# Two-branch cross-attention on one core: a new written-out order of all engines and transfers, and new softmax forms for ten of sixty score groups

## The chip, the core and the metric

The kernel runs on one core of a Trainium2 chip. The metric is device time in microseconds (us), median of the timed runs. The engines are TensorE (PE in the profile, its weight loads PEld), VectorE (DVE), ScalarE (ACT), GpSimd (POOL) and SyncE (SP), whose queue issues nearly all transfers.

## What is computed

For x of shape (2, 2048, 640) and a context of shape (2, 154, 1024), in float32, with 20 heads of 32 columns:

```
text, ip = context[:, :77], context[:, 77:]
q  = heads(x @ Wq.T)
o1 = softmax(q @ heads(text @ Wk.T).T / sqrt(32)) @ heads(text @ Wv.T)
o2 = softmax(q @ heads(ip @ Wk_ip.T).T / sqrt(32)) @ heads(ip @ Wv_ip.T)
out = merge(o1 + o2) @ Wo.T + bo + x
```

Each of the two softmaxes has 77 keys; their results are added ahead of the output projection.

## The kernel before

Everything is kept transposed, columns on partitions and tokens along the free dimension. The work of attention is cut into ten **pairs** (batch b, chunk c of 128 columns, that is four heads), numbered q = 5b + c, and each pair into two **units** of 1024 tokens, u = 0 to 19, so pair q has units 2q and 2q + 1. A unit's scores are made in three **groups** s of 3, 3 and 2 tiles of 128 tokens. A group of 3 tiles has 12 x 2 = 24 rows of softmax on each partition (tiles x heads x text or ip, 77 keys each), a group of 2 tiles has 16. All eight PSUM banks are used: scores and attention take four at a time (a half), everything else one.

The order of the whole program is written out by hand in one list of words, `SCHEDULE`. The program goes through it once and each word records its instructions; each engine then runs its own instructions in that order, and waits only for data and for buffers to come free. So a place in the list sets the order within an engine and within SP's queue, not a time. The words that matter here:

- `q.u.h` (TensorE) queries of half h of a unit, five matmuls of 512 columns into the bank behind the @; `cq.u.h` copies them out on ScalarE, scaled. `k`, `v`, `ck`, `cv`: the same for keys and values.
- `Rs.u` scores of a group; `Ks.u` copies them from PSUM to the SBUF tile `pb` (ScalarE, four copies, L245); `M` the row maximum (VectorE, L281); `S` subtracts it (GpSimd, L295); `E` exponential (ScalarE, L301); `D` row sums (VectorE, L306); `I` reciprocal; `N` normalise (GpSimd, L316); `T` transpose in 32 x 32 blocks (VectorE, L323).
- `A.q` attention of a pair, 80 small matmuls (L332), which need all six transposes of the pair and its V, and `CA.q` copies it to `aT` on ScalarE.
- `VS.q.half` spreads V of a pair into the tile `v4`, eight small copies from SBUF to SBUF on SP's queue (L158); `LX` loads a block of x (1280 KB), `LK` and `LQ` weights, `LO` Wo, `SF` and `SS` fetch x for the residual and store a part of the output.
- `m`, `o`, `cm`, `co`: output projection of batch 0 in seven products of 2 x 2 blocks, with sums of weights (`W`) and of tokens (`G`) on GpSimd ahead of them and adds from PSUM into the tile `acc` on VectorE behind them.
- `F0` to `F32`, `p`, `z`, `V`, `X`, `Y`, `yz`: output projection of batch 1, at the end. 33 products of sums, each in two halves (L848). `V.w.j.e` adds 128 x 128 weights and `X.w.e` adds 128 x 1024 tokens, on VectorE (e = d) or GpSimd (e = p); `Y` adds a bank to a part of the output (VectorE, L792 and L794). A product that adds to a bank, or begins a new chain in it, needs the `Y` that read it last.

Each group has one of several softmax forms, by three sets. In `DIRECT` there is no copy: the maximum and the exponential read PSUM, four reductions for `M` (L284). In `DIRECT` and in `BIASED` there is no subtraction: the exponential takes the maximum as its bias, which makes it one instruction a row (L269). In `SUMMED` the exponential also sums its row on ScalarE (one more instruction a row in the trace), and `D` is left out.

The opening (loads, seven warm-up matmuls, three queries and the keys of chunk 0) is written ahead of the list.

Of the kernel before, what the change touches and what calls it, by code (L numbers as in the profile page):

```python
# [9 lines left out]
F32 = mybir.dt.float32  # L10
# [10 lines left out]
def kernel(  # L21
# [43 lines left out]
        (11, 0), (13, 0), (13, 2), (14, 0), (14, 2), (15, 1), (15, 2), (16, 2), (18, 1),  # L65
    }
    BIASED = {
        (2, 2), (3, 2), (4, 2), (5, 2), (6, 2), (7, 2), (9, 2), (11, 2), (12, 0), (12, 2), (18, 2), (19, 0),
        (19, 2),
    }  # L70
    SUMMED = {
        (4, 2), (6, 2), (11, 2), (12, 0), (12, 2), (13, 0), (13, 2), (14, 0), (15, 1), (15, 2), (18, 1),
        (18, 2), (19, 2),
# [480 lines left out]
    for t in range(2):  # L554
# [216 lines left out]
    for c, stages in enumerate(chains_of):  # L771
        for _, text in stages:
            for _, t in terms(text):
                for h in range(NH):
                    o = int(t[0]), NH * int(t[1]) + h
# [115 lines left out]
```

## Time and profile before

| What | before |
| --- | --- |
| timed runs, median (lowest to highest) | 497.72 us (497.66 to 498.04) |
| span of the profiled execution | 496.7 us |
| TensorE busy | 490.3 us (99%) |
| VectorE busy | 408.5 us (82%) |
| GpSimd busy | 362.5 us (73%) |
| ScalarE busy | 315.0 us (63%) |
| moved by DMA | 69.38 MB, 140 GB/s in the mean |
| granted TensorE clock | 1.000 |

For the profiled execution the profile gives the span, from its first to its last instruction, and no separate device time; the 1.0 us between the span and the median of the timed runs lies around it. A busy share is an average over the span; a wait is listed with the instruction that ended it.

### The profile page before, as it was taken

The numbers are of one execution on the slowest core, as the hardware profiler recorded it, in microseconds if no ns is written. First come the engines' busy times: TensorE is split into PE (matmuls) and PEld (weight loads), VectorE is DVE, ScalarE is ACT, GpSimd is POOL, SyncE is SP. The second block draws the span as 40 slices with busy tenths as digits, with TensorE's granted clock in tenths as the row PEclk, the third lists the DMA queues.
The fourth block names the chain that finished last, engine by engine and source line by source line (L and its number), as shares of the span: only waits on it lengthen the run. The fifth ranks groups of instructions, "written<-read, shape, count | busy, mean of one in ns | idle before, by whom it ended". The sixth has DMA issues, their size and how long they took to land.

```text
span 496.7 us, 10482 instructions
## 1 busy us (share of the span) xinstructions
PE 490.3 (99%) x4114; PEld 287.9 (58%) x4114; DVE 408.5 (82%) x412; ACT 315.0 (63%) x1021; POOL 362.5 (73%) x157
## 2 busy tenths in 40 slices
PE   8999999999999999999999999999999999999997
PEld 5676657657547556456647654755755675444442
DVE  0069989979979989969976896687999978898877
ACT  1165878978978778668999786587578966100000
POOL 0069978798888999989874858565899888284830
PEclk9999999999999999999999999999999999999999
DMA  8991440332360454886445177418525401420115
GB/s 259 356 246 40 132 120 1 106 93 69 92 213 3 132 178 132 274 273 237 158 152 191 58 244 210 133 57 246 174 69 171 127 23 43 149 84 1 43 73 223
DMA packets 67474, 69.38 MB, mean 140 GB/s; under 512 B 5473, under 2 KB 47201, under 8 KB 67425
## 3 DMA queue, kind: packets, MB, share of 16 engines
q1 hardware_dynamic: 66704, 68.00, 43.8%
q8 instruction: 32, 0.52, 0.5%
q10 hardware_dynamic: 720, 0.72, 0.4%
q14 instruction: 18, 0.14, 0.1%
HBM read 54.94 MB, written 10.49 MB: 132 GB/s over the span
## 4 chain that ended last, share of the span: by engine, by line
PE 92%; DMA 3%; SPq 1%; DVE 1%; POOL 1%; ACT 1%; issue 0%; POOLq 0%
PE bank L201 33%; PE bank L848 11%; PE bank L490 10%; PE bank L233 10%; PE bank L332 10%; PE bank L142 9%; PE bank L471 6%; PE bank L500 3%; DMA aT<-in_L_xattn_Wk_ip_dram 2%; DMA wq<-in_L_xattn_Wq_dram 2%; SPq L534 1%; POOL pb L316 1%; DVE den L306 0%; ACT pb L301 0%; SPq L132 0%
## 5 line engine op out<-in xcount | busy, mean ns | idle before, releaser
L316 POOL TENSOR_TENSOR pb<-pb,rden 128x1848 f32<-128x1848 f32 (+1 forms) x60 | 176.1, 2944 | 39.7 <-DVE rden L311 35.5
L201 PE MATMUL bank<-x,wq 128*128 128x512 f32 x400 | 180.4, 601 | 0.6 <-DMA x<-in_x_dram 0.5
L295 POOL TENSOR_TENSOR pb<-pb,mx 128x1848 f32<-128x1848 f32 (+1 forms) x38 | 119.3, 3152 | 51.8 <-DVE mx L281 51.5
L201 PEld LDWEIGHTS bank<-x,wq 128*128 128x128 f32 x400 | 74.1, 191 | 86.7 <-issue 80.8
L323 DVE STREAM_TRANSPOSE pb<-pb 128x1920 f32<-128x1920 f32 (+1 forms) x60 | 115.7, 1932 | 4.9 <-POOL pb L316 4.3
L281 DVE TENSOR_REDUCE mx<-pb 128x24 f32<-128x1848 f32 (+1 forms) x51 | 93.7, 1850 | 30.7 <-ACT pb L245 30.5
L245 ACT COPY pb<-bank 128x462 f32<-128x462 f32 (+1 forms) x204 | 87.2, 539 | 36.0 <-PE bank L233 35.4
L306 DVE TENSOR_REDUCE den<-pb 128x24 f32<-128x1848 f32 (+1 forms) x47 | 88.7, 1895 | 17.6 <-ACT pb L301 13.3
L301 ACT ACTIVATE pb<-pb 128x1848 f32<-128x1848 f32 (+1 forms) x38 | 64.2, 1696 | 17.8 <-POOL pb L295 17.5
L269 ACT ACTIVATE pb<-pb,mx 128x77 f32<-128x77 f32 x224 | 67.8, 364 | 0.3 <-DVE mx L281 0.2
L233 PEld LDWEIGHTS bank<-kT,qT 32*128 32x128 f32 x1280 | 45.4, 184 | 26.9 <-issue 15.6
L269 ACT ACTIVATE pb<-bank,mx 128x77 f32<-128x77 f32 x184 | 51.8, 386 | 9.3 <-DVE mx L284 9.3
L233 PE MATMUL bank<-kT,qT 32*128 32x154 f32 x1280 | 56.2, 305 | 0.3 <-ACT kT L559 0.3
L332 PE MATMUL bank<-pb,v 32*32 32x512 f32 x1600 | 55.2, 597 | 0.0
L142 PE MATMUL bank<-wo_ct,aT 128*128 128x154 f32 x320 | 45.6, 296 | 0.3 <-DMA aT<-in_L_xattn_Wk_ip_dram 0.3
L142 PEld LDWEIGHTS bank<-wo_ct,aT 128*128 128x128 f32 x320 | 42.9, 188 | 3.6 <-issue 2.2
L332 PEld LDWEIGHTS bank<-pb,v 32*32 32x32 f32 x1600 | 29.9, 103 | 22.8 <-issue 10.7
L211 ACT ACTIVATE qT<-bank 128x512 f32<-128x512 f32 x40 | 24.2, 619 | 22.1 <-PE bank L201 22.0
L471 PE MATMUL bank<-aT,wo_ct 128*128 128x512 f32 x80 | 36.1, 596 | 0.0
L269 ACT ACTIVATION_READ_ACCUMULATOR pb<-bank,mx 128x1 f32 x128 | 33.6, 267 | 0.0
L490 PE MATMUL bank<-aT,wo_ct 128*128 128x256 f32 x128 | 32.3, 385 | 0.0
L490 PEld LDWEIGHTS bank<-aT,wo_ct 128*128 128x128 f32 x128 | 23.7, 190 | 6.5 <-issue 3.0
(75 smaller groups left out, 434.4 us busy)
## 6 DMA issues: line engine op xcount, KB each, us to landing
x<-in_x_dram SPq DMA_DIRECT2D x20, 1280.0 KB, 6.7
out_dram<-acc SPq DMA_DIRECT2D x20, 256.0 KB, 2.3
x<-in_x_dram SPq DMA_DIRECT2D x18, 256.0 KB, 5.9
acc<-in_x_dram SPq DMA_DIRECT2D x16, 256.0 KB, 4.7
out_dram<-x SPq DMA_DIRECT2D x15, 256.0 KB, 2.0
v<-vS SPq DMA_DIRECT2D x160, 20.0 KB, 2.8
wq<-in_L_xattn_Wq_dram SPq DMA_DIRECT2D x9, 320.0 KB, 5.0
aT<-in_L_xattn_Wk_dram SPq DMA_DIRECT2D x5, 512.0 KB, 5.5
```

The lines of the kernel that those rows point to most:

```text
L142: nc.tensor.matmul(keys_in(out), loaded[n][:, k, :], cT[:, k, :, t, :], start=(k == 0), stop=(k == NCC - 1))
L201: nc.tensor.matmul(pq, wqs[q % 3][:, k, :], xs[place_of(u, h)][:, k, :], start=(k == 0), stop=(k == NC - 1),)
L233: nc.tensor.matmul(ps[g][:, ts(t, 2 * L)], qTs[(u, h)][g * D : (g + 1) * D, ts(st, P)], kT[g * D : (g + 1) * D, c, b].rearrange("p t l -> ...
L245: nc.scalar.copy(keys_of(u, s)[:, :, g], ps[g][:, : n * 2 * L].rearrange("p (n l) -> p n l", n=n))
L269: nc.scalar.activation(row, row if ps is None else rows_in(ps[g], n)[:, t, x], AF.Exp, bias=maxs[(u, s)][:, *one], accum_out=None if den i ...
L281: nc.vector.tensor_reduce(mx, rows_of(u, s), AX.X, ALU.max, negate=negate)
L295: nc.gpsimd.tensor_tensor(rows_of(u, s), rows_of(u, s), maxs[(u, s)].unsqueeze(3).to_broadcast([P, n, 2, L]), ALU.subtract)
L306: nc.vector.tensor_reduce(den_of(u, s), rows_of(u, s), AX.X, ALU.add)
L316: nc.gpsimd.tensor_tensor(rows_of(u, s), rows_of(u, s), rdens[(u, s)].unsqueeze(3).to_broadcast([P, n, 2, L]), ALU.mult)
L323: nc.vector.transpose(p, p)
L332: nc.tensor.matmul(pa[r][g * D : (g + 1) * D, :], v4s[q % 2][rows, g, k, :], zones[rows, :, g, k, :], start=(k == 0), stop=(k == NK - 1),)
L490: nc.tensor.matmul(part, w_of[m][:, kp, op], t_of(m, b, i)[:, kp], start=(op == kp == 0 and m in (1, 2, 5)), stop=(op == 1 and kp == 1 and ...
```

## The change

The list is written in another order, and the three sets that choose the softmax forms are changed. The words that don't belong to a form are the same, with the same engine for each `V` and `X`; some words use another PSUM bank. Buffers, shapes and the code of every word are the same. The sets are one line shorter and the list two lines, so line numbers behind them are lower: L158 becomes L157, L186 L185, L245 L244, and, behind the list, L792 becomes L789, L794 L791, L828 L825, L834 L831 and L848 L845.

```
     DIRECT = {
-        (11, 0), (13, 0), (13, 2), (14, 0), (14, 2), (15, 1), (15, 2), (16, 2), (18, 1),
+        (11, 0), (13, 0), (13, 2), (14, 0), (14, 2), (15, 1), (16, 2), (18, 1),
     }
     BIASED = {
-        (2, 2), (3, 2), (4, 2), (5, 2), (6, 2), (7, 2), (9, 2), (11, 2), (12, 0), (12, 2), (18, 2), (19, 0),
-        (19, 2),
+        (3, 2), (4, 2), (5, 2), (6, 2), (7, 2), (9, 2), (11, 2), (12, 2), (14, 1), (15, 2), (18, 0), (18, 2),
+        (19, 0), (19, 2),
     }
     SUMMED = {
-        (4, 2), (6, 2), (11, 2), (12, 0), (12, 2), (13, 0), (13, 2), (14, 0), (15, 1), (15, 2), (18, 1),
-        (18, 2), (19, 2),
+        (4, 2), (11, 2), (12, 2), (15, 1), (15, 2), (18, 2), (19, 2),
     }
...
     SCHEDULE = (
-        "R0.0@1 R1.0@0 K0.0 q.1.0@4 LK.5 K1.0 M0.0 M1.0 S0.0 R2.0@0 v.0.0@6 K2.0 cq.1.0 S1.0 M2.0 E0.0 v.0.1@0 LK.6 "
...
+        "R0.0@1 K0.0 R1.0@0 K1.0 q.1.0@4 cq.1.0 LK.5 M0.0 R2.0@0 K2.0 v.0.0@7 q.1.1@5 M1.0 M2.0 S0.0 S1.0 E0.0 D0.0 "
```

A pair (u, s) in a set is a unit and a group. Three places show how the engines' rows move.

**First, ScalarE at the scores of units 13 and 14.** `qT_16_0` is a copied query, `mx_14_2` and `mx_14_0` are the maxima of two groups of unit 14. Before:

```order
L269 ACTIVATE pb_89<-bank_7_74,mx_14_2_2543 128x77 x4
L301 ACTIVATE pb_89<-pb_89 128x12x154
L245 COPY pb_89<-bank_4_71 128x3x154
L245 COPY pb_89<-bank_5_72 128x3x154
L245 COPY pb_89<-bank_6_73 128x3x154
L245 COPY pb_89<-bank_7_74 128x3x154
L211 ACTIVATE qT_16_0_2605<-bank_1_68 128x512
L269 ACTIVATE pb_89,den_14_0_2634<-bank_4_71,mx_14_0_2629 128x77 x6
```

Now:

```order
L268 ACTIVATE pb_89<-bank_7_74,mx_14_2_2510 128x77 x4
L244 COPY pb_89<-bank_4_71 128x3x154
L244 COPY pb_89<-bank_5_72 128x3x154
L244 COPY pb_89<-bank_6_73 128x3x154
L244 COPY pb_89<-bank_7_74 128x3x154
L300 ACTIVATE pb_89<-pb_89 128x12x154
L210 ACTIVATE qT_16_0_2599<-bank_1_68 128x512
L268 ACTIVATE pb_89<-bank_4_71,mx_14_0_2582 128x77 x6
```

The exponential of group (13, 1), the row with 128x12x154, now stands behind the four copies of group (14, 1), and the exponential of (14, 0) has lost its sums (`den`).

**Second, SP's queue between the attention of pairs 7 and 8.** `v4_0` is the tile for V of even pairs and `v4_1` for odd ones, `x_1` one of the tiles for x. Before:

```order
L186 DMA x_2_84<-in_x_dram 128x5x512
L158 DMA v4_0_80<-vS1_95 32x160 x8
L461 DMA acc_87<-in_x_dram 128x2x256
L186 DMA x_0_82<-in_x_dram 128x5x512
L461 DMA acc_87<-in_x_dram 128x2x256
L467 DMA out_0_dram<-acc_87 128x2x256
L158 DMA v4_1_81<-vS1_95 32x160 x16
L467 DMA out_0_dram<-acc_87 128x2x256
L465 DMA out_0_dram<-res_88 128x512
L186 DMA x_1_83<-in_x_dram 128x5x512
```

Now:

```order
L157 DMA v4_1_81<-vS1_95 32x160 x8
L466 DMA out_0_dram<-acc_87 128x2x256
L185 DMA x_1_83<-in_x_dram 128x5x512
L460 DMA acc_87<-in_x_dram 128x2x256
L157 DMA v4_1_81<-vS1_95 32x160 x8
L466 DMA out_0_dram<-acc_87 128x2x256
L460 DMA acc_87<-in_x_dram 128x2x256
L157 DMA v4_0_80<-vS1_95 32x160 x8
```

The second half of pair 8's V (`VS.8.0`, the row with v4_0) stood ahead of both halves of pair 9's; now it stands behind them and behind the last x load.

**Third, the sums at the end, VectorE.** L828 (now L825) is a `V`, L834 (now L831) an `X`, L792 (now L789) a first `Y` or `yz`, L794 (now L791) a later `Y`. Before, from the four sums X.U, X.T, X.S and X.W in a row on:

```order
L834 TENSOR_TENSOR pb<-aT 128x1024 x4
L792 SCALAR_TENSOR_TENSOR x_83<-x_83,bo_sb,bank_71 128x512
L828 TENSOR_TENSOR pb<-pb,wo_ct 128x128
L834 TENSOR_TENSOR pb<-aT 128x1024
L792 SCALAR_TENSOR_TENSOR x_84<-x_84,bo_sb,bank_67 128x512
L792 SCALAR_TENSOR_TENSOR x_82<-x_82,bo_sb,bank_69 128x512
L792 SCALAR_TENSOR_TENSOR acc<-acc,bo_sb,bank_68 128x512
L792 SCALAR_TENSOR_TENSOR x_84<-x_84,bo_sb,bank_70 128x512
L828 TENSOR_TENSOR pb<-pb,wo_ct 128x128 x2
```

Now, from X.U and X.W on (the single row L831 is X.T, and the last row, wo_ct,pb, is V.H):

```order
L831 TENSOR_TENSOR pb<-aT 128x1024 x2
L789 SCALAR_TENSOR_TENSOR acc<-acc,bo_sb,bank_68 128x512
L789 SCALAR_TENSOR_TENSOR x_83<-x_83,bo_sb,bank_71 128x512
L789 SCALAR_TENSOR_TENSOR x_84<-x_84,bo_sb,bank_67 128x512
L831 TENSOR_TENSOR pb<-aT 128x1024
L825 TENSOR_TENSOR pb<-pb,wo_ct 128x128
L789 SCALAR_TENSOR_TENSOR x_84<-x_84,bo_sb,bank_68 128x512
L789 SCALAR_TENSOR_TENSOR res<-res,bo_sb,bank_74 128x512
L789 SCALAR_TENSOR_TENSOR x_84<-x_84,bo_sb,bank_70 128x512
L789 SCALAR_TENSOR_TENSOR x_82<-x_82,bo_sb,bank_69 128x512
L825 TENSOR_TENSOR pb<-wo_ct,pb 128x128
```

The sum X.T now stands among the adds from banks, and V.H, which was done far ahead of them, follows four of them.

And GpSimd at the same place, before:

```order
L828 TENSOR_TENSOR pb<-wo_ct,pb 128x128
L834 TENSOR_TENSOR pb<-aT 128x1024
L828 TENSOR_TENSOR pb<-wo_ct 128x128 x2
L834 TENSOR_TENSOR pb<-pb,aT 128x1024
L834 TENSOR_TENSOR pb<-aT,pb 128x1024
L834 TENSOR_TENSOR pb<-aT 128x1024
```

Now:

```order
L825 TENSOR_TENSOR pb<-pb,wo_ct 128x128 x2
L831 TENSOR_TENSOR pb<-aT,pb 128x1024
L825 TENSOR_TENSOR pb<-wo_ct 128x128
L825 TENSOR_TENSOR pb<-pb,wo_ct 128x128 x2
L825 TENSOR_TENSOR pb<-wo_ct,pb 128x128
L831 TENSOR_TENSOR pb<-aT 128x1024
```

The sum X.L (aT,pb) was the third long one, behind X.M and X.P; now it is the first of them, and four small sums stand between it and X.M.

122 rows, old and new, of the table SCHEDULE are left out of this document.

## The prediction

> **What bounds the kernel now.** I read the page first, then the waits of TensorE, then the chain of work that ended last. The page's engine shares and the chain's shares:
>
> ```profile
> span 496.7 us, 10482 instructions
> PE 490.3 (99%) x4114; PEld 287.9 (58%) x4114; DVE 408.5 (82%) x412; ACT 315.0 (63%) x1021; POOL 362.5 (73%) x157
> PE 92%; DMA 3%; SPq 1%; DVE 1%; POOL 1%; ACT 1%; issue 0%; POOLq 0%
> ```
>
> TensorE is idle for 496.7 - 490.3 = 6.4 us in all. Its waits, every one that the profile lists:
>
> ```profile
> PE bank L549 <- DVE pb L547: 1.1, 1, 1.1
> PE bank L201 <- DMA x<-in_x_dram: 0.5, 1, 0.5
> PE bank L233 <- ACT kT L559: 0.3, 1, 0.3
> PE bank L142 <- DMA aT<-in_L_xattn_Wk_ip_dram: 0.3, 1, 0.3
> PE bank L490 <- DVE acc L515: 0.2, 1, 0.2
> ```
>
> The first four (2.2 us) lie in the opening, ahead of the first word of the order, and its code stays. Three pieces of the chain in order of time (start, duration, what):
>
> ```profile
> 24.41 1.96 PE bank L233 x48
> ...
> 442.24 50.77 PE bank L848 x118
> 493.03 0.69 DVE acc L794
> ```
>
> The order begins at 24.41 with the first scores and ends with the last product at 493.0; behind that stand one add, one store and the closing, 496.7 - 493.0 = 3.7 us, which the new order keeps (its last two words are the same). So of the 6.4 us idle, 2.2 + 3.7 = 5.9 are out of the change's reach: 0.5 us are left for an order to win. Inside the products TensorE is paced by itself: 118 records are 59 products, 50.77 / 59 = 0.860 us each. The span of 496.7 belongs to the profiled execution; the median of the timed runs is 497.72, 1.0 us longer, and I carry that 1.0 over.
>
> **The change on TensorE itself.** It has the same 231 words, in almost the same sequence: up to pair 9's attention some fifteen words are swapped with a neighbour or two, and behind it the products are reordered more freely. What a change of kind costs (a group of full-height matmuls behind scores or attention) could differ, so I counted: 50 such changes into full height, 50 out of it and 20 between scores, before and now. TensorE's own work: 0.
>
> **The softmax forms.** Durations by form:
>
> ```profile
> L316 POOL TENSOR_TENSOR pb<-pb,rden 128x1848 f32<-128x1848 f32 x40 | 131.3, 3288 | 24.8 <-DVE rden L311 22.7 <-ACT aT L355 1.1 <-ACT pb L245 0.6
> L295 POOL TENSOR_TENSOR pb<-pb,mx 128x1848 f32<-128x1848 f32 x33 | 108.3, 3289 | 51.8 <-DVE mx L281 51.5
> L323 DVE STREAM_TRANSPOSE pb<-pb 128x1920 f32<-128x1920 f32 x40 | 86.3, 2160 | 3.7 <-POOL pb L316 3.2
> L306 DVE TENSOR_REDUCE den<-pb 128x24 f32<-128x1848 f32 x35 | 72.1, 2060 | 14.0 <-ACT pb L301 13.3 <-ACT pb L269 0.6
> L281 DVE TENSOR_REDUCE mx<-pb 128x24 f32<-128x1848 f32 x35 | 71.5, 2051 | 28.4 <-ACT pb L245 28.3
> L301 ACT ACTIVATE pb<-pb 128x1848 f32<-128x1848 f32 x33 | 58.0, 1765 | 16.4 <-POOL pb L295 16.2
> 225.00:250.00 25.00, 24.92 (x168) 15.33 (x167) 24.93 (x23) 22.44 (x87) 23.50 (x13) 1.00 0.56 183
> ```
>
> Six groups lose their sums on ScalarE: (12,0), (13,0), (14,0), (18,1) of 24 rows cost VectorE 2.06 each, (6,2) and (13,2) of 16 rows two thirds of that, 1.4: 11.0 us. (15,2) trades four reductions from PSUM for one from SBUF, some 0.5 less. VectorE: +10.5, from 82% to 84% of the span. GpSimd gets the subtractions of (2,2) and (12,0) back (2.2 + 3.3) and loses those of (14,1) and (18,0) (2 x 3.3): -1.1. ScalarE loses six sets of sums and the row-by-row exponentials of (2,2) and (12,0), gains those of (14,1) and (18,0) and four copies for (15,2): less work in all, and it is idle for 182 us. None of this is on TensorE's path while the engines keep ahead of it. The cover is thin in places: in the window row above (columns: PE, PEld, DVE, ACT, POOL busy) VectorE works 24.93 of 25 us, and (12,0)'s new sum falls right behind that stretch. If the cover goes, a late sum delays normalise and transpose, and the pair's attention waits. I followed two such chains.
>
> **Pair 6's attention (first order listing).** ScalarE now copies the scores R1.14 ahead of the exponential E1.13, which was the other way round; VectorE takes the maximum M1.13 later.
>
> ```profile
> 283.72 3.57 ACT L269 ACTIVATE pb<-bank,mx 128x77 f32<-128x77 f32 x16 [1.43 <-DVE mx L284]
> 287.60 1.07 PE L233 MATMUL bank<-kT,qT 32*128 32x154 f32 x24
> 288.69 2.00 ACT L245 COPY pb<-bank 128x462 f32<-128x462 f32 x4
> 292.55 2.27 DVE L284 TENSOR_REDUCE mx<-bank 128x6 f32<-128x462 f32 x4
> 301.17 5.52 PE L332 MATMUL bank<-pb,v 32*32 32x512 f32 x160
> ```
>
> R1.14 is computed from 287.60, so its copies end near 288.4 + 1.9 = 290.3. M1.13 follows M2.14 and an add on VectorE, say 285.4 to 287.4; S1.13 on GpSimd 3.3, to 290.8; E1.13 then 1.8, to 292.6: the copy in front of it costs nothing, because E1.13 is waiting for S1.13 anyway. Its sum 2.1 and reciprocal: 294.9. From there N1.13 takes 3.3, to 298.2, while VectorE does M0.14 (2.3, to 297.2) and T2.13 (1.5, to 298.7); T1.13 2.2 ends at 300.9. At the same time E0.14, unsummed now (16 such rows took 3.57, so 24 take 5.3), runs from 295.5 to 300.8. The attention, which overwrites the same banks and needs the transpose, starts at 301.17: 0.3 us to spare. Bounds: 0 if the chain is as short as this, 1.0 us if each of the six steps begins 0.2 later. I take 0, with the nearest row.
>
> **Pair 8's values (second listing).** Of the sixteen copies that spread V of pair 8, the eight of VS.8.0 move on SP's queue from ahead of pair 9's to the far end: behind a store, an x load, a fetch, pair 9's eight copies, a store and a fetch, two of which wait for a store to land. Each DMA counts:
>
> ```profile
> 341.09 0.38 SPq L186 DMA_DIRECT2D x<-in_x_dram  x1
> 341.52 6.74 SPq L158 DMA_DIRECT2D v<-vS  x8
> 358.74 10.89 SPq L158 DMA_DIRECT2D v<-vS  x16
> 364.53 0.68 DVE L521 TENSOR_TENSOR acc<-acc,bank 128x512 f32<-128x512 f32 x1
> 388.65 5.54 PE L332 MATMUL bank<-pb,v 32*32 32x512 f32 x160
> x<-in_x_dram SPq DMA_DIRECT2D x20, 1280.0 KB, 6.7
> out_dram<-acc SPq DMA_DIRECT2D x20, 256.0 KB, 2.3
> v<-vS SPq DMA_DIRECT2D x160, 20.0 KB, 2.8
> ```
>
> Eight copies take 5.4 to issue, or until the load issued just ahead of them has landed (341.09 + 6.7 is the end of the 6.74 row). The store in front waits for the add that ended at 365.2; allow 366. The x load follows at 366.5 and lands at 373.2. The fetch waits for the store's landing, 368.3; pair 9's copies then run to 374.2; the next store 374.7; its fetch waits 2.3, to 377; pair 8's eight copies run to 382.9 and land at 385.7. The attention that reads them starts at 388.65: 3 us to spare. Cost 0; if the queue is more than 3 us later, TensorE waits for each us beyond.
>
> **The closing products (third listing).** Here VectorE and GpSimd both add pairs of SBUF tiles, and those wait for each other:
>
> ```profile
> 436.11 0.28 DVE L828 TENSOR_TENSOR pb<-pb,wo_ct 128x128 f32<-128x128 f32 x1
> 436.31 1.22 DVE L834 TENSOR_TENSOR pb<-aT 128x1024 f32<-128x1024 f32 x1
> 436.48 1.37 POOL L828 TENSOR_TENSOR pb<-wo_ct,pb 128x128 f32<-128x128 f32 x1 [7.57 <-DVE pb L828]
> 469.41 4.66 POOL L834 TENSOR_TENSOR aT<-aT 128x1024 f32<-128x1024 f32 x2
> 472.73 1.50 DVE L828 TENSOR_TENSOR pb<-pb,wo_ct 128x128 f32<-128x128 f32 x1
> 428.85 2.31 ACT L359 COPY aT<-bank 128x256 f32<-128x256 f32 x8 [10.84 <-POOL pb L828]
> ```
>
> The small sum at 472.73 is the kind that took 0.28 at 436.11; it ended 0.15 after GpSimd's long add (469.41 + 4.66 = 474.07). GpSimd's small one at 436.48 ended behind VectorE's long one (437.5). The Trainium skill states the rule in "SBUF — State Buffer", section "Who interferes with whom": a VectorE instruction with two SBUF inputs contends with a GpSimd one that reads SBUF, and whichever came first holds the port for its whole length. By that rule the trace agrees, 1.50 against 0.28.
> Before, VectorE's long adds stood mostly where GpSimd was idle. Now GpSimd's run of long adds is placed otherwise, and VectorE's small sum V.H comes up beside one. Worked out: pair 9's copies end at 431.2; behind them VectorE does three long adds and a small one to 435.4, and GpSimd, held up twice, starts its add X.L near 435.7 and reads to 438. VectorE's X.T is ready at 437.8 and ends at 439.2. Four small GpSimd sums later X.M runs from 440.8 to 443.1. V.H, behind one more small sum and four bank adds of 0.63, is ready at 442 and waits 1.1. Four more adds then end at 445.9. TensorE reaches product 29's second half, which needs the last of them, at 429.1 + 1.0 + 3.4 + 14 x 0.86 = 445.5: 0.4 late. Bounds: 0 if V.H slips in ahead of X.M; 1.5 if the chain ahead is 0.6 later and two more products wait. I take 0.4, the worked value.
>
> **The sum.** 0 (TensorE) + 0 (forms) + 0 (pair 6) + 0 (pair 8) + 0.4 (ports) - 0.1 (part of the 0.5 idle) = +0.3: 497.72 + 0.3 = 498.0. A change under 0.2% (1.0 us) can hardly be told from none here.
>
> **Rivals.** *Slower by the ports:* V.H and the small sums behind it wait longer, VectorE's adds fall behind and bank after bank comes free late. For it speaks that both long waits in the trace are of this kind; against it that the later products have 0.5 to 1.6 us of room. Upper bound 1.5 of waits at the first two products, 0.5 behind: up to 499.7; it decides from 1.0 us of TensorE waits behind 437 us. Chance 0.16.
> *Slower by a late queue:* pair 8's values, or another chain like pair 6's, come late. It decides when the SP queue is 4 us behind my working, or three chains slip by 0.35. Price 1 to 3 us: 498.7 to 500.7. Against it: margins of 3 and 0.3 us are positive. Chance 0.12.
> *Faster:* the order takes out the 0.5 us of idle time and also gaps under 0.15 us that no row lists. Even 1.0 us would need twice the listed idle time: 496.6. Chance 0.07. The Trainium skill ("Perfetto Trace Analysis", section "Identifying the Most-Contended Engine") warns that TensorE's busy share says little on how near it is to its peak, and to look at the load share, here 58%. By that rule there would be room; the 0.860 us of every product, whatever it reads, shows none that an order could use.
> *No change that can be measured* is the forecast: 0.65.
>
> **Numbers.** The range of 8 in 10 leaves out most of faster and the late part of both slower cases: 497.0 to 499.4. Faster 0.07, same 0.65, slower 0.16 + 0.12 = 0.28.
>
> **What would show it.** TensorE's busy share again 99% and its waits behind 24.4 us under 1 us in sum; pair 6's attention near 301.2 and pair 8's near 388.7, without a wait for a DMA; VectorE's busy time near 419 us, less what waits are counted in; small VectorE sums of over 1 us behind 440, and a TensorE wait for a VectorE bank add near 445. The prediction is wrong if TensorE waits for a DMA in the attention part, or if its waits in the products pass 1 us.

## The result, and the profile after

| | before | changed |
| --- | --- | --- |
| timed runs, median (lowest to highest) | 497.69 us (497.52 to 498.04) | 501.88 us (501.40 to 504.16) |
| ratio, 95% interval | | 1.009 (1.0075 to 1.0105) |
| profiled execution, span | 496.7 us | 500.4 us |

The changed kernel is slower by 4.2 us, that is by 0.75% to 1.05%. The forecast of 498.0, with a range from 497.0 to 499.4, was wrong; slower had a chance of 0.28 in it. The changed kernel's times also spread more, over 2.8 us against 0.5. All medians of this document leave out three executions at a much lower granted clock (716.62 us at 0.656 of the kernel before, 718.93 at 0.659 and 519.86 at 0.946 of two experiments), and the changed kernel's slowest run, 504.16, had a clock of 0.996 where its others had 0.999 or 1.000.

These are the head of the changed kernel's profile, one row of its part on DMA queues (packets, MB, share) and the chain's shares by engine, and then the longest waits of TensorE (us in total, times, longest):

```profile
span 500.4 us, 10364 instructions
PE 491.3 (98%) x4114; PEld 288.6 (58%) x4114; DVE 423.5 (85%) x415; ACT 306.8 (61%) x905; POOL 366.1 (73%) x157
q8 instruction: 32, 0.52, 0.4%
PE 85%; DVE 6%; DMA 3%; POOL 2%; issue 1%; SPq 1%; ACT 1%; DVEq 0%; POOLq 0%
```

```profile
PE bank L232 <- issue: 1.6, 2, 1.1
PE bank L845 <- DVE x L789: 1.6, 2, 1.1
PE bank L548 <- DVE pb L546: 1.1, 1, 1.1
```

TensorE has 85% of the chain where it had 92, VectorE 6 where it had 1. Its waits in the opening are of the same kind as before, and two rows are new: 1.6 us in scores (L232) that the profile puts down to "issue", that is to nothing it can name, and 1.6 us in the closing products (L845) for adds from banks on VectorE.

To find the places, each TensorE word is followed from one trace to the other. The changed kernel is behind the kernel before (minus: ahead of it) by this much at the start of a pair's attention: pair 0 -1.06 us, pair 1 -0.98, pair 2 +0.09, pair 3 +0.31, pair 4 +1.65, pair 9 +1.10, and at the end +3.7. The first -0.8 is the opening, the same code in both (first scores at 24.41 us before, 23.58 after). So the loss has three places: 1.1 us behind pair 1's attention, 1.3 behind pair 3's, and 2.6 in the closing products; between pairs 4 and 9 half a microsecond is won.

**Place one and two, the scores behind the attention of pairs 1 and 3.** TensorE and SyncE of the changed kernel in order of time (start, duration, what; in brackets the idle time before it):

```profile
105.89 5.52 PE L331 MATMUL bank<-pb,v 32*32 32x512 f32 x160
105.99 0.37 SPq L191 DMA_DIRECT2D wq<-in_L_xattn_Wq_dram  x1
106.41 0.52 SPq L131 DMA_DIRECT2D aT<-in_L_xattn_Wk_dram  x1
111.34 1.05 PE L232 MATMUL bank<-kT,qT 32*128 32x154 f32 x21
112.95 0.53 PE L232 MATMUL bank<-kT,qT 32*128 32x154 f32 x3 [0.55 <-issue]
...
179.26 5.52 PE L331 MATMUL bank<-pb,v 32*32 32x512 f32 x160
179.36 0.37 SPq L185 DMA_DIRECT2D x<-in_x_dram  x1
184.71 0.80 PE L232 MATMUL bank<-kT,qT 32*128 32x154 f32 x15
186.56 0.55 PE L232 MATMUL bank<-kT,qT 32*128 32x154 f32 x9 [1.05 <-issue]
```

TensorE stops inside one word: of the 24 records of R0.5, 21 run and three come later, and of R0.9 15 run and 9 come later. The operands of all 24 are the same copies, so no operand can have come late in their midst. Counted in the trace among all TensorE records, the record behind the first stop is number 1986 and that behind the second number 3521: 1535 apart, six times 256 less one. The row of queue q8 says what has such a period: 32 packets of kind "instruction", 0.52 MB, 16 KB each, for 8321 TensorE records (matmuls, weight loads and 93 others), so one for some 256. This says that TensorE's instructions come by DMA in packets of 256, here called pages; the experiments below test it. The trace has each packet's start and length. The table sets them beside the TensorE record with which a page begins (number 194 modulo 256, to within one):

```
us             page before   packet of    packet     next page   next page begins
               begins        next page    has        begins      after landing
                             starts       landed
before,  pair 1   108.22        109.05      110.19      113.08       2.89
before,  pair 3   180.22        182.54      183.68      185.03       1.35
changed, pair 1   107.24        110.44      111.60      112.95       1.35
changed, pair 3   180.50        184.01      185.04      186.57       1.53
```

In these four rows a page's packet starts 0.8 to 3.5 us after the page ahead begins (where matmuls are long it can be ahead of that, by up to 7.4 us in the trace of before), and in the last three, where the page is only just in time or late, it is used 1.35 to 1.53 us after it has landed. Attention and scores use up a page in 4.7 to 4.9 us when nothing stops them. In the changed kernel the packets start 3.2 and 3.5 us after the page ahead begins. In the 1.3 us before that, 832 KB of weights and 1280 KB of x were issued (the SPq rows). In the kernel before it is 0.8 and 2.3 us.

**Place three, the closing products.** VectorE, GpSimd and TensorE of the changed kernel:

```profile
435.57 2.35 DVE L831 TENSOR_TENSOR pb<-aT 128x1024 f32<-128x1024 f32 x2
435.73 3.03 POOL L825 TENSOR_TENSOR pb<-pb,wo_ct 128x128 f32<-128x128 f32 x2 [5.90 <-DVE pb L825]
438.72 2.35 POOL L831 TENSOR_TENSOR pb<-aT,pb 128x1024 f32<-128x1024 f32 x1
439.81 2.35 DVE L831 TENSOR_TENSOR pb<-aT 128x1024 f32<-128x1024 f32 x1
443.72 2.34 POOL L831 TENSOR_TENSOR pb<-aT 128x1024 f32<-128x1024 f32 x1
443.86 1.40 DVE L789 SCALAR_TENSOR_TENSOR x<-x,bo_sb,bank 128x512 f32<-128x512 f32 x2
445.17 1.04 DVE L825 TENSOR_TENSOR pb<-wo_ct,pb 128x128 f32<-128x128 f32 x1
445.31 1.12 PE L845 MATMUL bank<-pb 128*128 128x512 f32 x2 [1.11 <-DVE x L789]
446.93 1.13 PE L845 MATMUL bank<-pb,wo_ct 128*128 128x512 f32 x2 [0.49 <-DVE x L789]
```

The GpSimd row at 435.73 holds two sums, V.U.2 (2.50 us; VectorE's X.U and X.W, the row at 435.57, are over at 437.92) and V.V.0 (0.45). So X.L starts only at 438.72, and X.T (439.81), a sum of 1.22 us by itself, takes 2.35 and ends 1.1 us after X.L. Six VectorE instructions later V.H (445.17) takes 1.04 us instead of 0.28; it ends just behind GpSimd's X.M (443.72). F20.1, the second half of product 20, waits for the second of the two adds at 443.86, which stand behind X.T, and F7.1 for the add behind V.H. Against the step of 0.86 us the losses are 1.27 at F20.1, 0.76 at F7.1, and 0.1 to 0.2 at five halves of products behind: 2.6 us.

### The profile page after: what moved, and what is told of

Same layout as the page of the kernel before. It is cut to its first block, busy times and chain, and to the rows that moved or that the text cites. A ratio compares the mean times of both kernels' runs of the same rounds, so it can differ in the third digit from the quotient of the medians.

```text
span 500.4 us, 10364 instructions
## 1 busy us (share of the span) xinstructions
PE 491.3 (98%) x4114; PEld 288.6 (58%) x4114; DVE 423.5 (85%) x415; ACT 306.8 (61%) x905; POOL 366.1 (73%) x157
## 4 chain that ended last, share of the span: by engine, by line
PE 85%; DVE 6%; DMA 3%; POOL 2%; issue 1%; SPq 1%; ACT 1%; DVEq 0%; POOLq 0%
PE bank L200 33%; PE bank L232 10%; PE bank L845 10%; PE bank L331 10%; PE bank L489 9%; PE bank L141 9%; PE bank L470 4%; PE bank L499 2%; DMA aT<-in_L_xattn_Wk_ip_dram 2%; DMA wq<-in_L_xattn_Wq_dram 1%; DVE pb L831 1%; POOL pb L315 1%; DVE x L789 1%; DVE den L305 1%; SPq L533 1%
## 5 line engine op out<-in xcount | busy, mean ns | idle before, releaser
L280 DVE TENSOR_REDUCE mx<-pb 128x24 f32<-128x1848 f32 (+1 forms) x52 | 95.4, 1844 | 35.9 <-ACT pb L244 35.9
L305 DVE TENSOR_REDUCE den<-pb 128x24 f32<-128x1848 f32 (+1 forms) x53 | 99.8, 1886 | 17.0 <-ACT pb L300 16.2
L244 ACT COPY pb<-bank 128x462 f32<-128x462 f32 (+1 forms) x208 | 88.5, 537 | 32.1 <-PE bank L232 31.6
L268 ACT ACTIVATE pb<-pb,mx 128x77 f32<-128x77 f32 x248 | 72.0, 373 | 3.2 <-DVE mx L280 3.2
L232 PEld LDWEIGHTS bank<-kT,qT 32*128 32x128 f32 x1280 | 45.6, 184 | 27.0 <-issue 16.3
L232 PE MATMUL bank<-kT,qT 32*128 32x154 f32 x1280 | 56.7, 305 | 1.9 <-issue 1.6
L268 ACT ACTIVATE pb<-bank,mx 128x77 f32<-128x77 f32 x168 | 39.0, 388 | 10.0 <-DVE mx L283 10.0
L791 DVE TENSOR_TENSOR x<-x,bank 128x512 f32<-128x512 f32 x36 | 23.9, 684 | 4.3 <-PE bank L845 3.6
```

The lines of the kernel that those rows point to most:

```text
L232: nc.tensor.matmul(ps[g][:, ts(t, 2 * L)], qTs[(u, h)][g * D : (g + 1) * D, ts(st, P)], kT[g * D : (g + 1) * D, c, b].rearrange("p t l -> ...
L244: nc.scalar.copy(keys_of(u, s)[:, :, g], ps[g][:, : n * 2 * L].rearrange("p (n l) -> p n l", n=n))
L268: nc.scalar.activation(row, row if ps is None else rows_in(ps[g], n)[:, t, x], AF.Exp, bias=maxs[(u, s)][:, *one], accum_out=None if den i ...
L280: nc.vector.tensor_reduce(mx, rows_of(u, s), AX.X, ALU.max, negate=negate)
L305: nc.vector.tensor_reduce(den_of(u, s), rows_of(u, s), AX.X, ALU.add)
```

## The experiments

Each experiment moves words of the changed kernel's list and nothing else, unless it is said otherwise. Times are medians; the kernel before, timed again beside each, had 497.6 to 497.7 us.

**The transfers alone.**

```
- q.5.1@2 S0.4 LK.14 LQ.5 E0.4 cq.5.1 A.1@1 ... LK.12 ... VS.2.0 M2.6
+ q.5.1@2 S0.4 LK.14 LK.12 E0.4 cq.5.1 A.1@1 ... VS.2.0 LQ.5 M2.6
- LX.11.0 LX.10.1 I2.8 v.4.1@5 VS.5.0
+ LX.11.0 I2.8 v.4.1@5 VS.5.0 LX.10.1
```

> The changed kernel with three transfers moved on SyncE's queue and nothing else: the weights LK.12 ahead of LQ.5, LQ.5 behind pair 2's first spread of V, and the x block LX.10.1 behind VS.5.0, so that none of them is issued in the first microsecond of the attention of pairs 1 and 3. Theory (instruction pages): TensorE's instructions come in pages of 256 by the same DMA engines; the page asked for 1.3 us into such an attention queues behind the fresh loads, lands 4.3 to 4.5 us after it was asked for instead of 2 to 3, and the scores R0.5 and R0.9 stop at the page's end for 1.1 and 1.4 us. Without the loads both stops go: 2.2 us less than the changed kernel, about 499.6. Rival (data): R0.5 and R0.9 wait for banks or operands that the new order of ScalarE and VectorE brings late; none of the three transfers feeds them, so no change, 501.9.

Measured: 499.80 us (499.44 to 500.14), 2.1 less than the changed kernel. TensorE's waits:

```profile
PE bank L845 <- DVE x L789: 1.6, 2, 1.1
PE bank L548 <- DVE pb L546: 1.1, 1, 1.1
PE bank L232 <- ACT kT L558: 0.3, 1, 0.3
```

The row with "issue" is gone, the one of the closing stays. The packets now start 0.9 us after the page ahead begins, in both places, and land 2.6 and 2.7 us before the next page is used.

**The reverse, on the kernel before.**

```
- LK.14 LK.11 M0.4 R1.4@1 q.5.1@1 T1.3
+ LK.14 M0.4 R1.4@1 q.5.1@1 LQ.5 LK.11 T1.3
- I2.5 LQ.5 ck.3.0
+ I2.5 ck.3.0
- K1.8 SF.0.2 T1.7 ... M0.9 LX.10.1 R2.9@0
+ K1.8 SF.0.2 LX.10.1 T1.7 ... M0.9 R2.9@0
```

> The reverse, on the kernel before: LQ.5 and LK.11 issued right behind pair 2's last queries, just ahead of pair 1's attention, and LX.10.1 right behind the queries that free its tile, just ahead of pair 3's; nothing else moves. Theory (instruction pages): the pages asked for at the start of these attentions now queue behind 832 and 1280 KB, land about 3 us or more after they were asked for (0.8 and 2.3 before), and R0.5 and R0.9 stop for about 1 us each: 498.6 to 499.6 where the kernel before has 497.6. Rival (data): earlier loads can only help or do nothing: 497.6.

Measured: 500.10 us, ratio 1.0047 (1.0034 to 1.006), 2.4 us slower, somewhat more than expected.

```profile
106.21 0.37 SPq L192 DMA_DIRECT2D wq<-in_L_xattn_Wq_dram  x1
106.64 0.52 SPq L132 DMA_DIRECT2D aT<-in_L_xattn_Wv_ip_dram  x1
112.85 0.53 PE L233 MATMUL bank<-kT,qT 32*128 32x154 f32 x3 [0.24 <-issue]
...
179.04 0.37 SPq L186 DMA_DIRECT2D x<-in_x_dram  x1
186.54 0.53 PE L233 MATMUL bank<-kT,qT 32*128 32x154 f32 x5 [1.11 <-issue]
```

The kernel before gets the same stops at the same instruction numbers, to within one. From pair 1's attention to pair 2's it loses 0.75 us against its own trace, from pair 3's to pair 4's 1.62, and nothing elsewhere. The packets land 1.28 and 1.32 us before the next page begins. Three transfers issued earlier cost 2.4 us, with no operand late: the data rival is out.

**Half a page more ahead.** Two runs put 128 TensorE instructions more into the opening, so that pages end elsewhere in the program.

```
- for _ in range(7):
-     nc.tensor.matmul(banks[0][:, :P], warm, warm, start=True, stop=True)
+ for _ in range(39):
+     nc.tensor.matmul(banks[0][:32, :32], warm[:32, :32], warm[:32, :32], start=True, stop=True)
```

> The changed kernel with 39 warm-up products of 32x32 by 32x32 in place of 7 of 128x128 by 128x128. Nothing else differs: all orders and all transfers stay, but every later TensorE instruction stands 128 places further on, half a page of 256. Theory (instruction pages): the pages' ends leave R0.5 and R0.9 and fall about 128 instructions earlier, into the queries or the attention itself; the page that is used up fastest is then asked for before the loads are issued. The stops of 1.1 and 1.4 us in R0.5 and R0.9 vanish; unless another page takes their place, 499.5, and any stop that is left lies a multiple of 256 instructions from the others, at a new place. Rival (data): both stops stay where they are, and the time with them, 501.9 plus or minus what the other warm-up does to the opening (0.5).

Measured: 504.39 us (504.04 to 505.19). Both expectations missed the time, and there is no trace of these runs that could tell why, so this experiment decides nothing. Then the large products came back:

```
+ for _ in range(32):
+     nc.tensor.matmul(banks[0][:32, :32], warm[:32, :32], warm[:32, :32], start=True, stop=True)
  for _ in range(7):
```

> The changed kernel with 32 small warm-up products (32x32 by 32x32) ahead of the 7 large ones, which stay: 128 TensorE instructions more, the clock warmed as before, all orders and transfers unchanged, and an opening that is 1 to 2 us longer. Theory (instruction pages): the stops in R0.5 and R0.9, which lie 6 pages of 256 apart, leave their places, since the pages now end half a page earlier in the program, in the queries ahead of the attention, and asked for before the loads are issued; about 1 to 2.5 us of stops less, and 1 to 2 of opening more. A stop that remains lies 128 instructions off the old ones, modulo 256. Rival (data): both stops stay in R0.5 and R0.9.

Measured: 505.97 us in one run, with an opening 2.0 us longer (pair 0's attention at 70.77 against 68.71). From there to pair 3's attention it keeps the distance to the kernel before, +0.99 to +1.16, and it keeps it to pair 4's (+1.33): the stops in R0.5 and R0.9 are gone. There is one stop without a named cause, inside pair 4's attention:

```profile
209.71 0.41 SPq L185 DMA_DIRECT2D x<-in_x_dram  x1
212.90 4.90 PE L331 MATMUL bank<-pb,v 32*32 32x512 f32 x134
218.88 1.13 PE L331 MATMUL bank<-pb,v 32*32 32x512 f32 x26 [1.07 <-issue]
```

The record behind it is number 4290, nine times 256 behind number 1986. The packet of that page started 3.4 us after the page ahead began, while 1284 KB of data were moved, and landed 1.46 us ahead of its use. No order of data has changed, and the stop has gone where the page's end went; the packets are 33 now, for 8449 records.

The time is worse than expected. In the traces it is 3.8 us more than the changed kernel: 2.1 more in the opening, 2.2 less in the two places, 1.6 more between the attention of pairs 4 and 5, and 2.3 more in the closing. There, just behind the two stops for VectorE, the granted clock was 0.5 for 3.4 us (from 448.70 on), and the products F29.0 and F29.1 lost 0.75 and 0.85 us where the changed kernel's lost 0.1 each. Why the clock fell here and not behind the same stops in the changed kernel's trace, no run settles.

**The closing: two words moved.**

```
- F20.0 X.L.p@9 V.V.1.d V.M.0.p ... Y6.1.10 V.H.0.d yz.1 ... Y2.1.31 F29.0 V.W.0.p V.S.0.d
+ F20.0 V.V.1.d V.M.0.p ... Y6.1.10 yz.1 ... Y2.1.31 V.H.0.d F29.0 V.W.0.p X.L.p@9 V.S.0.d
```

> The changed kernel with two words of the closing products moved and the same work: GpSimd's long sum X.L behind four small sums, just ahead of X.M, and VectorE's small sum V.H behind five adds from banks. Theory (shared port): X.T (2.35 us where 1.22 is its own length) and V.H (1.04 instead of 0.28) no longer meet GpSimd's long adds, VectorE's adds come 1.1 us earlier at F20.1 and 1.9 us earlier at F7.1; both stops of TensorE go, and the steps of 0.95 behind them: 2.2 us less, 499.7. Rival (backlog): VectorE simply has too many sums ahead of its adds from banks; the order of GpSimd changes nothing, and 0.28 us of V.H is all that goes: 501.6.

Measured: 500.16 us, 1.7 less than the changed kernel; the profile still has a stop of 1.55 us in R0.9 and only 0.2 us of waits for VectorE. As the pages' stops differ between traces (0.55 and 1.05 us in the changed kernel's, one of 1.55 here), the words were also moved on top of the first experiment's kernel.

> The changed kernel with both edits at once: the three transfers of the first experiment out of the attention's start, and the two words of the closing products moved. Theory (pages and port, two separate causes that add up): 499.8 of the first experiment less 1.6 to 2.3 of the closing = 497.5 to 498.2, level with the kernel before, with no stop in R0.5 and R0.9 and none at F20.1 and F7.1. Rival (something else in the new order or in the softmax forms costs time as well): 0.5 us or more above the kernel before is left, and TensorE shows waits elsewhere.

Measured: 497.95 us, ratio to before 1.0004 (0.9995 to 1.0013). TensorE's waits behind the opening:

```profile
PE bank L845 <- DVE x L789: 0.2, 1, 0.2
```

The losses against the step of 0.86 are 0.5 us in all where the changed kernel has 2.6. One after the other the edits take out 2.1 and 1.85 us, 3.9 of 4.2, and the rest can't be told from nothing. The moved words take out nearly as much with the pages' stops (1.7) as without them (1.85), so the two causes stand side by side.

**V.H alone**, on the changed kernel and then on the first experiment's.

```
- Y6.1.10 V.H.0.d yz.1 ... Y2.1.31 F29.0
+ Y6.1.10 yz.1 ... Y2.1.31 V.H.0.d F29.0
```

> The changed kernel with VectorE's small sum V.H alone moved behind five adds from banks; GpSimd's order is as in the changed kernel. Theory (shared port): the stop at F20.1 stays at 1.1 us, because the add that it needs stands ahead of V.H and behind X.T; the stop at F7.1 and the slower steps behind it go, since V.H no longer waits for X.M: 0.8 to 1.0 us less, 501.0. Rival (backlog): 0.28 us less at most, 501.6.

Measured: 501.82 us (500.93 to 504.36), not separable from the changed kernel, because the runs of both scatter over more than the effect; what makes them scatter stays open, since one run of each was traced. The trace has the stop at F20.1 (1.10 us) and none at F7.1.

> The first experiment's kernel (499.8), with VectorE's small sum V.H alone moved behind five adds from banks. Theory (shared port): the stop at F20.1 stays at 1.1 us, that at F7.1 goes, since V.H no longer waits for GpSimd's X.M: 0.8 to 1.0 us less, 498.9. Rival (VectorE has too much ahead of its adds, and the port adds nothing): 0.28 us less at most, 499.5.

Measured: 499.05 us, 0.75 less: nearly the 0.8 to 1.0 of the shared port and well over the rival's 0.28. The stop at F20.1 is there as before (1.10 us), the 0.49 at F7.1 is not:

```profile
442.99 1.12 PE L845 MATMUL bank<-pb 128*128 128x512 f32 x2 [1.10 <-DVE x L789]
443.95 1.02 PE L845 MATMUL bank<-pb,wo_ct 128*128 128x512 f32 x2
```

**X.L alone**, on the first experiment's kernel; VectorE's order is untouched.

```
- F20.0 X.L.p@9 V.V.1.d ... V.W.0.p V.S.0.d
+ F20.0 V.V.1.d ... V.W.0.p X.L.p@9 V.S.0.d
```

> The first experiment's kernel (499.8), with GpSimd's long sum X.L alone moved behind four small sums, just ahead of X.M; VectorE's order is untouched. Theory (shared port): X.T takes about 1.25 instead of 2.35 us, the stop of 1.1 us at F20.1 goes, and V.H waits for one of the two long GpSimd sums for 0.2 to 1.0 us: 1.2 to 1.8 less, 498.0 to 498.6. Rival (VectorE has too much ahead of its adds): its work and its order are the same, so no change, 499.8.

Measured: 497.94 us, 1.9 less, a little more than expected. X.T and V.H on VectorE, and X.L on GpSimd:

```profile
437.80 1.28 DVE L831 TENSOR_TENSOR pb<-aT 128x1024 f32<-128x1024 f32 x1
441.83 0.45 DVE L825 TENSOR_TENSOR pb<-wo_ct,pb 128x128 f32<-128x128 f32 x1
439.77 2.36 POOL L831 TENSOR_TENSOR pb<-aT,pb 128x1024 f32<-128x1024 f32 x1
```

VectorE's work and order are the same, and 1.9 us go because one long sum of GpSimd starts 3.1 us later (counted from pair 9's attention): VectorE's load alone is not the cause. Moving V.H as well gains nothing more (497.95 with both words), so the two effects of 1.9 and 0.75 don't add up: with X.L moved, V.H takes 0.45 us and hardly waits.

**The heads and tails exchanged.** First the kernel before up to pair 9's last transpose, and the changed kernel's order behind it (forms as before):

> The kernel before up to the last transpose of pair 9, forms included, and the changed kernel's order behind it. Theory (the closing order is a cause of its own): the stops at F20.1 and F7.1 of about 1.1 and 0.5 us and the slower steps behind them, 2.0 to 2.6 us in sum: 499.6 to 500.2. Rival (VectorE comes into the closing late because of the 10 us of added sums in the attention part): without these sums the closing costs less than 0.5 us, 497.6 to 498.1.

Measured: 498.62 us, ratio 1.0017 (1.0008 to 1.0027), 0.9 us slower: less than half of what the theory gave, and more than the rival's 0.5. The port's waits are there (X.T 1.88, V.H 1.05 us), and one stop:

```profile
PE bank L850 <- DVE x L794: 0.5, 1, 0.5
```

Here VectorE comes out of the last transpose 0.5 us ahead of pair 9's attention, in the changed kernel 0.06 us ahead, and the next sums are not held up by GpSimd (V.T.0 0.47 against 1.05 us); so the add that F20.1 needs is in time. The stop of 1.27 us in the changed kernel needs both, the meeting with X.L (without it, under the same head, there is no stop at F20.1) and a VectorE that comes late from the attention part. Then the opposite, the first experiment's head with the closing order of before behind it:

> The changed kernel's order and softmax forms up to the last transpose of pair 9, with the three transfers moved as in the first experiment, and behind it the order of the kernel before, whose closing products have no stop of TensorE. Theory (two causes, nothing else; the new forms and the new attention part cost nothing): 497.3 to 497.8, at or just under the kernel before; the profile shows no wait behind the opening over 0.3 us. Rival (the new attention part or its added sums bring VectorE into the closing later, and that costs time under any closing order): 498.2 or more, with a wait for VectorE between 440 and 450 us.

Measured: 498.83 us, ratio 1.0025 (1.0016 to 1.0034). The theory's 497.3 to 497.8 missed, and the rival had the time and the wait right. GpSimd, VectorE and TensorE:

```profile
429.94 7.55 POOL L829 TENSOR_TENSOR pb<-pb,wo_ct 128x128 f32<-128x128 f32 x3 [3.11 <-DVE pb L829]
431.73 4.62 DVE L835 TENSOR_TENSOR pb<-aT 128x1024 f32<-128x1024 f32 x4
440.97 1.13 PE L849 MATMUL bank<-pb 128*128 128x512 f32 x2 [1.14 <-DVE acc L793]
```

V.U.2, the first of the three GpSimd rows, came up at 429.94, when VectorE had begun its run of sums without a gap, and ended at 436.66: 6.72 us for a sum that takes 0.45. In the kernel before it is done at 428.1, ahead of the run. Counted from the start of pair 9's attention, the add that TensorE waits for ends 2.1 us later than before. VectorE comes out of the last transpose 0.45 us later, its first sum takes 1.47 us instead of 0.35 beside a long one of GpSimd, and later it waits 0.52 for a GpSimd sum that stands behind V.U.2. So the late head and the port have a part in it together. The rival's "under any closing order" goes too far: the same head with the two words moved runs level with the kernel before (497.95).

**Three more small sums moved**, on the kernel with both edits:

```
- X.J.d@4 V.R.0.d Y6.1.21 ... Y7.1.21 V.W.1.d ... Y7.0.21 V.S.1.d ... F13.0 V.M.1.d F2.0
+ X.J.d@4 V.R.0.d V.W.1.d V.S.1.d V.M.1.d Y6.1.21 ... Y7.1.21 ... Y7.0.21 ... F13.0 F2.0
```

> The kernel with both edits (497.95), and three of VectorE's small sums (V.W.1, V.S.1, V.M.1) moved up behind V.R.0, into a stretch in which GpSimd has no long add. Theory (shared port): the three take 0.28 us each instead of 0.91, 1.18 and 1.12; of the 0.4 to 0.5 us that TensorE still loses at F24.0 and F13.0 most goes: 497.5, at or just under the kernel before. Rival (these waits cost nothing, since nothing that TensorE needs stands behind them): 497.95.

Measured: 497.69 us, ratio to before 1.0004 (0.9995 to 1.0013). The three sums take 0.29 us each, as expected, and the loss at F24.0 is shorter by 0.2 us. The median is 0.26 lower, but the ratio to the kernel before beside it is the same 1.0004, so theory and rival can't be told apart. No version here beats the kernel before; three are level with it.

## Why the prediction was wrong, step by step

*What bounds the kernel.* That TensorE's stream sets the time, and that only 0.5 us could be won, held. But the step "TensorE's own work: 0" took the stream as given. It had no term for what feeds TensorE with instructions, and no rival for it: the waits of before show none, since there the pages came in time (at pair 3 with the same 1.35 us as in a stop). The sign "TensorE waits for a DMA in the attention part" came true only in this hidden form. This omitted term is 2.1 us by the first experiment. The transfers were costed by their readers alone, at pair 8; the ones that cost time are others, which nobody was waiting for. A smaller misreading is the 1.0 us carried over from the span: each timed run here is 1.7 to 1.9 us longer than its own span, so the traced execution of before was itself some 0.8 us slower than the median. It moves nothing in the sum.

*The softmax forms: 0.* With the two causes taken out, the changed forms run level with before (1.0004), so by themselves they cost nothing that can be measured. But the same closing order lost 1.2 us in the trace behind the old head and 2.6 behind the new one. The head thus has a share in the loss at the closing; whether through the forms or through the order, no run separates. The 24-row sums went from 35 to 39:

```profile
L305 DVE TENSOR_REDUCE den<-pb 128x24 f32<-128x1848 f32 x39 | 80.4, 2061 | 16.4 <-ACT pb L300 16.2
```

VectorE was busy for 423.5 us where 419 was forecast; sums held up by GpSimd, which count as busy, are in it: with both edits it is 421.3, with the three small sums moved as well 419.4.

*Pair 6 and pair 8: 0.* Right. Their attention, without idle time ahead of it:

```profile
302.74 5.52 PE L331 MATMUL bank<-pb,v 32*32 32x512 f32 x160
389.72 5.52 PE L331 MATMUL bank<-pb,v 32*32 32x512 f32 x160
```

It starts later than the forecast 301.2 and 388.7 by what was lost earlier; with both edits it starts at 300.40 and 387.37. No wait of TensorE for a transfer of data is listed there.

*The closing products: 0.4.* The mechanism was right and the size wrong: 2.6 us in the trace, of which moving two words takes away 2.1 (1.85 in the medians). The step that failed is "GpSimd, held up twice, starts its add X.L near 435.7". It started at 438.72. Of these 3.0 us, 1.1 are the delay with which pair 9's attention began, and 1.9 are the closing's own. The row quoted from before shows a small GpSimd sum that waits for one long add; V.U.2 ahead of X.L waited for two that follow each other without a gap (2.50 us), and in the exchanged tail for a whole run (6.72). From there all shifted: X.T met X.L, which the working had nearly past each other, and the first product to stop was F20.1, not F29.1, where 0.1 us was lost. V.H's wait behind X.M, forecast at 1.1 us, measured 0.8. A wait for a bank add near 445 was named in advance and came, at 445.31, but at another product and behind another sum: that the times agree is luck.

*The rivals.* Slower by the ports (0.16) was the nearest: it was to decide from 1.0 us of TensorE waits behind 437 us, and there are 1.6. It gave at most 499.7, and could not reach 501.9 without the pages. The sign "its waits in the products pass 1 us" was the right one for this part; the one on transfers named no page of instructions. The opening, set at no change, differs by up to 1.5 us between profiles of the same code (first scores from 22.9 to 24.4 us), more than the 0.2% on which the chances were split.

## What to carry to other kernels

When all engines look hidden and TensorE's program is long, look at its instruction pages. Keep large transfers out of the microsecond or two in which a stretch of many short matmuls begins, because the next page comes late behind them, and read "issue" at distances of a multiple of 256 in the instruction count as the sign. Where VectorE and GpSimd hold each other up, place the sums by runs, not one by one: a short GpSimd sum that came up inside a run of VectorE sums waited here for the rest of the run. An order that is level by its sums can be 1% apart by such meetings, so compare orders with these two alone undone before judging the rest.

## What the hardware showed that was not expected

TensorE's instructions came in 32 packets of 16 KB, one for 256 instructions, and landed late when transfers of 0.8 to 1.3 MB were issued just ahead. At the two places the packet then started 2.7 to 4.2 us after the page ahead began (the changed kernel, the reverse and the experiments that leave the loads), against 0.7 to 1.3 in the first experiment and the five kernels built on it. The Trainium skill ("Runtime: NRT & Kernel Launch", section "Instruction fetch mechanics") states blocks of 16 KiB, that is 256 instructions, fetched in sequence over a DMA queue of the sequencer's own. By that the trace agrees. It also calls the crossing mostly hidden and gives TensorE room for 2048 instructions; here the page that had just landed was the next to be used, and TensorE stopped for up to 1.55 us at such a crossing.

GpSimd was kept out by VectorE for 6.72 us. The Trainium skill ("SBUF — State Buffer", section "Who interferes with whom") gives the port to whoever issues first, for the whole instruction; in this trace the hold went over several VectorE sums in a row.
